# Attention logits from bfloat16 rows that hold three-part splits of the sums, in place of float32 products of diagonals

## The chip, the cores and the metric

The kernel runs on one core of a Trainium2 chip. The metric is the device time of one execution in microseconds (us); a kernel's time is the median of its runs.

In the lines of the profile PE is TensorE (matrix products), DVE VectorE, ACT ScalarE and POOL GpSimd. A line of a timeline gives start and duration in us, engine, source line (L), operation, `output<-inputs`, shapes, and the number of records (x2) that it gathers; `[... <-...]` is the idle time ahead of it, the *idle column*, and what ended it.

## The reference, cut to what matters

Two graph layers over 128 graphs of 64 nodes with 768 features. The change concerns the attention logits of the second layer (6 heads of 128 features):

```python
th = jnp.tanh(h)                                        # h: per head, nodes x 128
attn_src = jnp.einsum('bhno,hoz->bhnz', th, w_src)      # one sum per node and head
attn_dst = jnp.einsum('bhno,hoz->bhnz', th, w_dst)
attn = attn_src + jnp.swapaxes(attn_dst, -1, -2)        # node n, neighbour m
attn = jnp.where(attn >= 0, attn, leaky_alpha * attn)
attn = jnp.where((adj == 0)[:, None, :, :], NEG_MASK, attn)   # NEG_MASK = -999
attn = jax.nn.softmax(attn, axis=-1)
...                                                     # weighted sum, elu, gate
```

So a logit is the sum of a source sum (of the row's node) and a destination sum (of the column's node). The question is how to get 128 x 384 such logits for each tile of two graphs.

## The kernel before

Layer 0 takes the first 1555 us; but for some small constants and transfers it is the same in both kernels. Layer 1 runs over 32 pairs of 128-row tiles. In each of its periods TensorE does the 42 large steps of one pair, each a float32 product with 384 columns, and the small steps of the pair before it are slipped in by step number:

```python
def merged(main, side):            # side steps go in ahead of main step n
    side = sorted(side, key=lambda e: e[0])
    i = 0
    for n, step in enumerate(main):
        while i < len(side) and side[i][0] <= n:
            side[i][1]()
            i += 1
        step()
    ...
```

The steps that the argument touches, with cuts marked by dots:

```python
def heads(t):
    th = work.tile([P, H, DO], F32, name="th")
    nc.scalar.activation(th, HS[t][:, :, :DO], AF.Tanh)
    sd = SD[t] = small.tile([P, 2, H], F32, name="sd")
    for h in range(H):                                   # six destination sums, DVE
        no = work.tile([P, DO], F32, name="no", bufs=1)
        nc.vector.scalar_tensor_tensor(no, th[:, h, :], 1.0, wsd[:, 1, h*DO:(h+1)*DO],
                                       op0=OP.mult, op1=OP.mult,
                                       accum_out=sd[:, 1, h : h + 1])
    dg = PB[t] = work.tile([P, H, N], F32, name="dg")
    for h in range(H):                                   # six diagonals, ACT
        nc.scalar.activation(dg[:, h, :], idc, AF.Copy, scale=sd[:, 1, h : h + 1])
    pr = work.tile([P, H, DO], F32, name="pr", bufs=1)   # source sums: POOL, then DVE
    nc.gpsimd.tensor_mul(pr, th, wsd[:, 0, :].rearrange("p (h o) -> p h o", h=H))
    nc.vector.tensor_reduce(sd[:, 0, :], pr, AX.X, OP.add)

def softmax(t):
    pl = pss.tile([P, H, N], F32, name="ps")
    nc.tensor.matmul(pl, blk, PB[t], start=True, stop=True)      # float32
    a = work.tile([P, H, N], F32, name="a")
    for h in range(H):
        nc.scalar.activation(a[:, h, :], pl[:, h, :], AF.Prelu,
                             bias=SD[t][:, 0, h : h + 1], alpha=LEAKY)
    nc.vector.copy_predicated(a, ...mask..., ...neg...)
    ...                                                  # maximum, subtraction, exp

def final(t, c0=0, c1=D):                                # the "closing operations": four on DVE, 768 columns
    nc.scalar.activation(e, f, AF.Exp, bias=mone)
    nc.vector.scalar_tensor_tensor(f, e, 1.0, f, op0=OP.min, op1=OP.max)
    ...

def behind(p):                                           # (main step, what)
    return [(0, lambda: heads(t0)), (3, lambda: heads(t1)), ...
            (13, lambda: softmax(t0)), (19, lambda: softmax(t1)),
            (24, lambda: turn_p(t0, 0)), ... (39, lambda: final(t1))]
```

Of the kernel before, what the change touches and what calls it, by code (L numbers as in the profile page):

```python
# [8 lines left out]
F32 = mybir.dt.float32  # L9
BF16 = mybir.dt.bfloat16  # L10
I32 = mybir.dt.int32
AF = mybir.ActivationFunctionType
OP = mybir.AluOpType
AX = mybir.AxisListType

P = 128
# [6 lines left out]
def kernel(  # L23
# [106 lines left out]
    ident = const.tile([P, P], F32, name="ident")  # L130
    make_identity(nc, ident)

    blk = const.tile([P, P], F32, name="blk")
    nc.vector.memset(blk, 0.0)

    idc = const.tile([P, N], F32, name="idc")
    for g in range(GT):
        s = slice(g * N, (g + 1) * N)
        nc.vector.memset(blk[s, s], 1.0)
        nc.vector.tensor_copy(idc[s, :], ident[s, s])  # L140
    mhalf = const.tile([P, 1], F32, name="mhalf")
    nc.vector.memset(mhalf, -0.5)

    def stats(src, to, behind=False):

# [62 lines left out]
    with ExitStack() as px:  # L208
# [42 lines left out]
        nc.sync.dma_start(wrt[:, 1, :], wrr_t)  # L251
        identb = wa.tile([P, P], BF16, name="identb")
        nc.vector.tensor_copy(identb, ident)
        blkb = wa.tile([P, P], BF16, name="blkb")
        nc.vector.tensor_copy(blkb, blk)

        vals = wa.tile([P, NG, N], BF16, name="vals")
        nc.gpsimd.iota(vals, pattern=[[1, NG], [0, N]], base=1, channel_multiplier=0,
# [244 lines left out]
        def finish(p):  # L503
            for k in range(2):
                t = 2 * p + k
                to = small.tile([P, 2], F32, name="rn")
                stats(X[t], to)
                h = keep.tile([P, D], F32, name="hf", bufs=2)
                nc.scalar.activation(h, X[t], AF.Relu, scale=to[:, 0:1], bias=to[:, 1:2])
                nc.sync.dma_start(H1D[p][k * P : (k + 1) * P, :], h)  # L510
                nc.gpsimd.tensor_add(X[t], X[t], h)
                nc.sync.dma_start(XH1[p][k * P : (k + 1) * P, :], X[t])
# [40 lines left out]
                (50, lambda: count_t(0, 0)), (50, lambda: count_t(0, 1))]  # L553
        for p in range(NP):
            more = [(3, lambda: finish(p - 1))] if p else late
            if p == NP - 1:
                more += fetch()
            merged(main(p), side(p + 1) + more)


    with ExitStack() as px:
# [16 lines left out]
        def load_x(p):  # L578
            for k in range(2):
                t = 2 * p + k  # L580
                XH[t] = work.tile([P, D], F32, name="x", bufs=4)
                nc.sync.dma_start(XH[t], XH1[p][k * P : (k + 1) * P, :])

        load(0)
# [6 lines left out]
        nc.sync.dma_start(wsd[:, 0, :], row(w_src, P))  # L591
        nc.sync.dma_start(wsd[:, 1, :], row(w_dst, P))
        nc.vector.tensor_scalar(bb, bb, 1.0, None, op0=OP.add)
        neg = wb.tile([P, N], F32, name="neg")
        nc.gpsimd.memset(neg, NEG_MASK)
        mone = wb.tile([P, 1], F32, name="mone")
        nc.gpsimd.memset(mone, -1.0)
        pbds = []
# [2 lines left out]
            nc.gpsimd.memset(pb, 0.0)  # L601
            pbds.append(pb)

        HS, Z, SD, PB = {}, {}, {}, {}
        A11, A12, A22, S1, S2, S3, S4 = {}, {}, {}, {}, {}, {}, {}

        def turn(p, k, h):
# [107 lines left out]
        def heads(t):  # L715

            th = work.tile([P, H, DO], F32, name="th")
            nc.scalar.activation(th, HS[t][:, :, :DO], AF.Tanh)  # L718
            sd = SD[t] = small.tile([P, 2, H], F32, name="sd")
            for h in range(H):  # L720
                no = work.tile([P, DO], F32, name="no", bufs=1)
                nc.vector.scalar_tensor_tensor(no, th[:, h, :], 1.0, wsd[:, 1, h * DO : (h + 1) * DO],  # L722
                                               op0=OP.mult, op1=OP.mult,
                                               accum_out=sd[:, 1, h : h + 1])
            dg = PB[t] = work.tile([P, H, N], F32, name="dg")
            for h in range(H):
                nc.scalar.activation(dg[:, h, :], idc, AF.Copy, scale=sd[:, 1, h : h + 1])  # L727
            pr = work.tile([P, H, DO], F32, name="pr", bufs=1)
            nc.gpsimd.tensor_mul(pr, th, wsd[:, 0, :].rearrange("p (h o) -> p h o", h=H))  # L729
            nc.vector.tensor_reduce(sd[:, 0, :], pr, AX.X, OP.add)  # L730

        def gate(t):

            nc.scalar.activation(Z[t], Z[t], AF.Tanh, scale=0.5)

        def mask(p):

            nc.vector.tensor_scalar(AI[p], AI[p], 0.0, None, op0=OP.is_equal)

        def softmax(t):  # L740

            p, k = divmod(t, 2)
            pl = pss.tile([P, H, N], F32, name="ps")
            nc.tensor.matmul(pl, blk, PB[t], start=True, stop=True)
            a = work.tile([P, H, N], F32, name="a")
            for h in range(H):
                nc.scalar.activation(a[:, h, :], pl[:, h, :], AF.Prelu,
                                     bias=SD[t][:, 0, h : h + 1], alpha=LEAKY)
            nc.vector.copy_predicated(a, AI[p][:, k, None, :].to_broadcast([P, H, N]),
                                      neg[:, None, :].to_broadcast([P, H, N]))  # L750
            mx = small.tile([P, H], F32, name="mx")
            nc.vector.tensor_reduce(mx, a, AX.X, OP.max)
            nc.vector.tensor_sub(a, a, mx[:, :, None].to_broadcast([P, H, N]))
            pb = PB[t] = pbds[t % 2]
            for g in range(GT):
                s = slice(g * N, (g + 1) * N)
                nc.scalar.activation(pb[s, :, s], a[s], AF.Exp)
# [3 lines left out]
        def turn_p(t, q):  # L761
            if q == 0:
                PT[t] = work.tile([P, H, P], F32, name="pT")
            ps = pss.tile([P, KH, P], F32, name="ps")
            for i in range(HH):
                nc.tensor.transpose(ps[:, i, :], PB[t][:, HH * q + i, :], ident)
            nc.scalar.copy(PT[t][:, HH * q : HH * q + HH, :], ps)
# [3 lines left out]
        def attend(t, q):  # L771

            if q == 0:
                FF[t] = work.tile([P, D], F32, name="f")
            po = pss.tile([P, HH, W], F32, name="ps")
            for i in range(HH):
                h = q * HH + i
                nc.tensor.matmul(po[:, i, :], PT[t][:, h, :], HS[t][:, h, :], start=True, stop=True)  # L778
            ri = small.tile([P, HH, 1], F32, name="ri")
            nc.vector.reciprocal(ri, po[:, :, DO : DO + 1])  # L780
            for i in range(HH):
                h = q * HH + i
                nc.vector.scalar_tensor_tensor(FF[t][:, h * DO : (h + 1) * DO], po[:, i, :DO],  # L783
                                               ri[:, i, :], bb, op0=OP.mult, op1=OP.add)
# [24 lines left out]
        def behind(p):  # L809

            if p < 0:
                return []
            t0, t1 = 2 * p, 2 * p + 1
            return [(0, lambda: heads(t0)),
                    (3, lambda: heads(t1)),
                    (5, lambda: load_x(p)),
                    (6, lambda: mask(p)),
                    (6, lambda: gate(t0)),
                    (7, lambda: gate(t1)),
                    (13, lambda: softmax(t0)),  # L820
                    (19, lambda: softmax(t1)),
                    (24, lambda: turn_p(t0, 0)),
                    (26, lambda: turn_p(t0, 1)),
                    (28, lambda: attend(t0, 0)),
                    (30, lambda: attend(t0, 1)),
                    (31, lambda: final(t0)),
                    (32, lambda: turn_p(t1, 0)),
                    (34, lambda: turn_p(t1, 1)),
                    (36, lambda: attend(t1, 0)),
                    (38, lambda: attend(t1, 1)),  # L830
                    (39, lambda: final(t1))]

        def last():


            p = NP - 1
            t0, t1 = 2 * p, 2 * p + 1
            steps = [(21, lambda: heads(t0)),
                     (21, lambda: heads(t1)),
                     (21, lambda: load_x(p)),  # L840
                     (21, lambda: mask(p)),
                     (28, lambda: softmax(t0)),
                     (35, lambda: softmax(t1)),
                     (40, lambda: turn_p(t0, 0)),
                     (40, lambda: turn_p(t0, 1)),
                     (41, lambda: attend(t0, 0)),
                     (41, lambda: attend(t0, 1)),
                     (99, lambda: gate(t0)),
                     (99, lambda: gate(t1))]
            for q in range(2):  # L850
                steps.append((99, lambda q=q: final(t0, q * HALF, (q + 1) * HALF)))
            for q in range(2):
                steps.append((99, lambda q=q: turn_p(t1, q)))
            for q in range(2):
                steps.append((99, lambda q=q: attend(t1, q)))
                steps.append((99, lambda q=q: final(t1, q * HALF, (q + 1) * HALF)))
            return steps
# [55 lines left out]
```

## Time and profile before

| Before | value | how to read it |
|---|---|---|
| time | 2677.28 us (2676.42 to 2678.2) | median of the runs that stand beside the changed kernel |
| TensorE busy | 2620.3 of a 2674.7 us span, 98% | the bound, but its records overlap: only starts can be subtracted |
| period of layer 1 | 34.33 us, 2003.38 to 2037.71 | the same transpose, one pair later |

The lines behind this, and TensorE's waits, are in the prediction.

### The profile page before, as it was taken

What the parts mean: (1) busy time and instruction counts of PE and PEld (TensorE: products, weight loads), DVE (VectorE), ACT (ScalarE), POOL (GpSimd) and SP (SyncE); (2) the same over time, 40 slices, a digit from 0 to 9 for tenths busy, and PEclk for the clock granted to TensorE, in tenths of its full rate; (3) what the DMA queues carried; (4) which work ended last, traced back from release to release, by engine and by line L of the source; (5) the groups of instructions that cost most, each with busy time, mean ns of one, the idle gap of its engine ahead of it and who ended that gap; (6) DMA issues with size and microseconds to landing.
All of it is one profiled execution on the core that took longest, in us unless ns stands there. A gap on an engine that the chain in (4) does not pass through costs nothing.

```text
span 2674.7 us, 29599 instructions
## 1 busy us (share of the span) xinstructions
PE 2620.3 (98%) x10348; PEld 1607.3 (60%) x10348; DVE 1810.1 (68%) x4240; ACT 843.2 (32%) x1892; POOL 612.6 (23%) x657
## 2 busy tenths in 40 slices
PE   6999999999999999999999999999999999999997
PEld 3566566665656656566665566666666666666664
DVE  7865565655646566564655258888888888888878
ACT  1111111111211112121111035555555555555554
POOL 2332222323123232222322221111111111111111
PEclk9999999999999999999999999999999999999998
DMA  5121121211112111121211322222222222222211
GB/s 179 40 75 38 40 73 38 75 38 51 62 38 75 38 65 48 38 75 38 75 36 40 134 86 73 73 73 74 73 73 70 66 68 72 71 65 68 72 61 48
DMA packets 91211, 173.47 MB, mean 65 GB/s; under 512 B 32958, under 2 KB 41521, under 8 KB 91062
## 3 DMA queue, kind: packets, MB, share of 16 engines
q1 hardware_dynamic: 90908, 171.52, 19.4%
q8 instruction: 82, 1.34, 0.2%
q14 instruction: 67, 0.55, 0.1%
q10 hardware_dynamic: 154, 0.06, 0.0%
HBM read 95.67 MB, written 75.50 MB: 64 GB/s over the span
## 4 chain that ended last, share of the span: by engine, by line
PE 71%; DVE 19%; ACT 6%; issue 3%; DMA 1%; SPq 0%; POOL 0%; ACTq 0%; DVEq 0%
PE pwa L451 20%; PE pwb L451 14%; PE pwd L451 7%; PE pwc L451 7%; PE pma L641 5%; PE pb L407 5%; PE pmc L641 5%; DVE no L722 4%; PE pmb L641 3%; DVE f L793 2%; ACT e L792 2%; DVE f L794 2%; DVE f L795 2%; DVE f L783 2%; PE ps L778 2%
## 5 line engine op out<-in xcount | busy, mean ns | idle before, releaser
L451 PE MATMUL pwa<-bwT,s 128*128 128x384 f32 x1152 | 391.1, 489 | 0.4 <-DVE x L468 0.4
L451 PEld LDWEIGHTS pwa<-bwT,s 128*128 128x128 f32 x1152 | 215.1, 190 | 145.4 <-issue 7.4
L641 PE MATMUL pma<-bvT,s 128*128 128x384 f32 x768 | 289.1, 487 | 0.0
L432 POOL TENSOR_TENSOR s<-s,a 128x384 f32<-128x384 f32 x96 | 95.7, 1022 | 644.8 <-PE pwa L451 597.7
L729 POOL TENSOR_TENSOR pr<-th,wsd 128x768 f32<-128x768 f32 x64 | 137.1, 2142 | 418.7 <-ACT th L718 211.2
L468 DVE TENSOR_TENSOR x<-pwa,x 128x384 f32<-128x384 f32 x128 | 69.5, 543 | 206.7 <-PE pwa L451 170.7
L451 PE MATMUL pwb<-bw,s 128*128 128x384 f32 x576 | 201.5, 489 | 0.0
L451 PE MATMUL pwb<-bwT,s 128*128 128x384 f32 x576 | 199.0, 491 | 0.0
L419 ACT COPY a<-pb 128x768 f32<-128x768 f32 x96 | 73.7, 800 | 392.1 <-PE pb L407 392.1
L451 PE MATMUL pwa<-bw,a 128*128 128x384 f32 x576 | 196.8, 490 | 0.0
L451 PE MATMUL pwc<-bw,a 128*128 128x384 f32 x576 | 191.6, 487 | 0.0
L451 PE MATMUL pwd<-bwT,a 128*128 128x384 f32 x576 | 191.3, 486 | 0.0
L396 ACT COPY cntT<-pb 117x128 bf16<-117x128 bf16 (+1 forms) x128 | 27.8, 269 | 484.4 <-PE pb L394 484.4
L727 ACT ACTIVATE dg<-idc,sd 128x64 f32<-128x64 f32 x384 | 128.6, 345 | 124.1 <-DVE no L722 123.8
L407 PE MATMUL pb<-r,h 64*128 64x192 f32 x1536 | 154.4, 341 | 13.2 <-ACT h L316 6.7
L407 PEld LDWEIGHTS pb<-r,h 64*128 64x128 f32 x1536 | 125.2, 190 | 69.2 <-issue 53.0
L641 PEld LDWEIGHTS pma<-bvT,s 128*128 128x128 f32 x768 | 131.5, 191 | 52.6
L722 DVE SCALAR_TENSOR_TENSOR no<-th,wsd 128x128 f32<-128x128 f32 x384 | 152.6, 397 | 5.6 <-ACT th L718 0.9
L451 PEld LDWEIGHTS pwc<-bw,a 128*128 128x128 f32 x576 | 109.8, 191 | 77.1 <-issue 1.5
L451 PEld LDWEIGHTS pwd<-bwT,a 128*128 128x128 f32 x576 | 109.4, 190 | 76.2 <-issue 0.2
L451 PEld LDWEIGHTS pwa<-bw,a 128*128 128x128 f32 x576 | 106.9, 192 | 69.4 <-issue 8.4
L451 PEld LDWEIGHTS pwb<-bwT,s 128*128 128x128 f32 x576 | 106.2, 190 | 69.0 <-issue 6.7
(139 smaller groups left out, 4625.4 us busy)
## 6 DMA issues: line engine op xcount, KB each, us to landing
x<-in_x_dram SPq DMA_DIRECT2D x64, 384.0 KB, 3.7
h<-hf SPq DMA_DIRECT2D x64, 384.0 KB, 3.0
xh<-x SPq DMA_DIRECT2D x64, 384.0 KB
h<-h SPq DMA_DIRECT2D x64, 384.0 KB, 3.0
x<-xh SPq DMA_DIRECT2D x64, 384.0 KB, 3.6
out_dram<-f SPq DMA_DIRECT2D x62, 384.0 KB, 2.6
ai<-in_adj_dram SPq DMA_DIRECT2D x64, 64.0 KB, 2.0
ai<-in_adj_t_dram SPq DMA_DIRECT2D x32, 64.0 KB, 3.4
```

Source lines behind the costliest of these rows:

```text
L407: nc.tensor.matmul(ps[:, g, i * 3 * N : (i + 1) * 3 * N], H0[t][s, kb * P : (kb + 1) * P], rts[p % 2][s, k].rearrange("p s n -> p (s n)"), ...
L419: nc.scalar.copy(A1[p][:, q].rearrange("p h s (g n) -> p g (h s) n", g=GT), pv)
L432: nc.gpsimd.tensor_sub(S2[p][:, q], S1[p][:, q], A1[p][:, q, 0])
L451: nc.tensor.matmul(bank[b][:, :HALF], a()[:, q, s, :], bw[w][s][:, q, :], start=(first and q == s == 0), stop=(q == KH - 1 and s == 2), sk ...
L468: nc.vector.tensor_add(v, bank[b][:, :HALF], v)
L641: nc.tensor.matmul(bank[b, s][:, :HALF], a[p][:, q, :], bv[w][s][:, q, :], start=(first and q == 0), stop=(q == KH - 1), skip_group_check= ...
L722: nc.vector.scalar_tensor_tensor(no, th[:, h, :], 1.0, wsd[:, 1, h * DO : (h + 1) * DO], op0=OP.mult, op1=OP.mult, accum_out=sd[:, 1, h : ...
L727: nc.scalar.activation(dg[:, h, :], idc, AF.Copy, scale=sd[:, 1, h : h + 1])
L729: nc.gpsimd.tensor_mul(pr, th, wsd[:, 0, :].rearrange("p (h o) -> p h o", h=H))
L778: nc.tensor.matmul(po[:, i, :], PT[t][:, h, :], HS[t][:, h, :], start=True, stop=True)
L783: nc.vector.scalar_tensor_tensor(FF[t][:, h * DO : (h + 1) * DO], po[:, i, :DO], ri[:, i, :], bb, op0=OP.mult, op1=OP.add)
L792: nc.scalar.activation(e, f, AF.Exp, bias=mone)
```

## The change

The intent: the float32 logits product costs TensorE four times a bfloat16 one, and ACT spends 12 small instructions per tile on diagonals and biases. Both sums are instead split into three bfloat16 parts (copy, subtract, copy, subtract, copy: three bfloat16 mantissas hold a float32 one), turned into rows by a small bfloat16 product, and one bfloat16 product of 82 rows adds source and destination sums in the float32 accumulator. The mask is done the other way round: a tile is filled with -999 and the edge matrix selects the logits into it. The core of the diff (cuts marked; constants, nine small transfers in layer 0, the order of the last pair and a smaller number of `x` buffers left out):

```diff
 def heads(t):
-            sd = SD[t] = small.tile([P, 2, H], F32, name="sd")
+            pr = work.tile([P, H, DO], F32, name="pr", bufs=1)
+            nc.gpsimd.tensor_mul(pr, th, wsd[:, 0, :]...)          # now first in line
             for h in range(H):
                 ...                                                # six sums on DVE, as before
-            dg = PB[t] = work.tile([P, H, N], F32, name="dg")
-            for h in range(H):
-                nc.scalar.activation(dg[:, h, :], idc, AF.Copy, scale=sd[:, 1, h : h + 1])
-            pr = ...; nc.gpsimd.tensor_mul(pr, ...)
-            nc.vector.tensor_reduce(sd[:, 0, :], pr, AX.X, OP.add)
+            nc.vector.tensor_reduce(sg[:, 2, :], pr, AX.X, OP.add)
+            nc.gpsimd.tensor_mul(sg[:, :GT, :], sd[...], gm[...])
+            sb = sdb[t % 2]
+            for i in range(NPART):                                 # NPART = 3
+                q = sb[:, :, i * H : (i + 1) * H]
+                nc.gpsimd.tensor_copy(q, sg)
+                if i < NPART - 1:
+                    nc.gpsimd.tensor_sub(sg, sg, q)
+        def rows(t):
+            nc.tensor.matmul(ps[:NR, : N + P], sdb[t % 2]..., idr, start=True, stop=True)
+            nc.vector.tensor_mul(rrow[t % 2][: 2 * HB], ps[...], de[: 2 * HB])
+            nc.scalar.copy(lrow[t % 2][2 * HB :], ps[2 * HB : NR, N : N + P])
         def softmax(t):
-            nc.tensor.matmul(pl, blk, PB[t], start=True, stop=True)
-            ...six Prelu with bias, copy_predicated with neg...
+            a = work.tile([P, H, N], F32, name="a")
+            nc.gpsimd.memset(a, NEG_MASK)
+            nc.tensor.matmul(pl, lrow[t % 2], rrow[t % 2], start=True, stop=True)
+            nc.scalar.activation(al, pl, AF.Prelu, alpha=LEAKY)
+            nc.vector.copy_predicated(a, AI[p]..., al)
 def behind(p):
-                    (6, lambda: mask(p)),
-                    (13, lambda: softmax(t0)),
-                    (19, lambda: softmax(t1)),
-                    (24, lambda: turn_p(t0, 0)), ...
+                    (12, lambda: rows(t0)),
+                    (15, lambda: softmax(t0)),
+                    (18, lambda: rows(t1)),
+                    (21, lambda: softmax(t1)),
+                    (25, lambda: turn_p(t0, 0)), ...               # the rest one step later
```

More of the change, by code (lines that the diff above doesn't have):

```diff
@@ L131 @@
     make_identity(nc, ident)
-    blk = const.tile([P, P], F32, name="blk")
-    nc.vector.memset(blk, 0.0)
     idc = const.tile([P, N], F32, name="idc")
@@ L138 @@
         s = slice(g * N, (g + 1) * N)
-        nc.vector.memset(blk[s, s], 1.0)
         nc.vector.tensor_copy(idc[s, :], ident[s, s])
@@ L142, with row_constants @@
     nc.vector.memset(mhalf, -0.5)
+    NPART = 3
+    HB = 32
+    NR = 2 * HB + NPART * H
+    assert NPART * H <= HB
+    dl = const.tile([P, H], F32, name="dl")
+    nc.gpsimd.memset(dl, 0.0)
+    def row_constants():
+        for c in range(3):
+            for i in range(NPART):
+                a = c * HB + i * H
+                nc.sync.dma_start(dl[a : a + H, :], ident[0:H, 0:H])
     def stats(src, to, behind=False):
@@ L254 @@
         blkb = wa.tile([P, P], BF16, name="blkb")
-        nc.vector.tensor_copy(blkb, blk)
+        nc.vector.memset(blkb, 0.0)
+        for g in range(GT):
+            s = slice(g * N, (g + 1) * N)
+            nc.vector.memset(blkb[s, s], 1.0)
         vals = wa.tile([P, NG, N], BF16, name="vals")
@@ L555 @@
             more = [(3, lambda: finish(p - 1))] if p else late
+            if p == 1:
+                more.append((10, row_constants))
             if p == NP - 1:
@@ L580, in load_x @@
                 t = 2 * p + k
-                XH[t] = work.tile([P, D], F32, name="x", bufs=4)
+                XH[t] = work.tile([P, D], F32, name="x", bufs=3)
                 nc.sync.dma_start(XH[t], XH1[p][k * P : (k + 1) * P, :])
@@ L593 @@
         nc.vector.tensor_scalar(bb, bb, 1.0, None, op0=OP.add)
-        neg = wb.tile([P, N], F32, name="neg")
-        nc.gpsimd.memset(neg, NEG_MASK)
         mone = wb.tile([P, 1], F32, name="mone")
@@ L602 @@
             pbds.append(pb)
-        HS, Z, SD, PB = {}, {}, {}, {}
+        de = wb.tile([P, H, N], BF16, name="de")
+        nc.gpsimd.tensor_copy(de, dl[:, :, None].to_broadcast([P, H, N]))
+        idr = wb.tile([P, N + P], BF16, name="idr")
+        nc.gpsimd.tensor_copy(idr[:, :N], idc)
+        nc.gpsimd.tensor_copy(idr[:, N:], ident)
+        gm = wb.tile([P, GT], F32, name="gm")
+        nc.gpsimd.memset(gm, 0.0)
+        for g in range(GT):
+            nc.gpsimd.memset(gm[g * N : (g + 1) * N, g : g + 1], 1.0)
+        lrow, rrow, sdb = [], [], []
+        for i in range(2):
+            sb = wb.tile([P, 3, HB], BF16, name=f"sdb{i}")
+            nc.gpsimd.memset(sb, 0.0)
+            sdb.append(sb)
+            rr = wb.tile([NR, H, N], BF16, name=f"rrow{i}")
+            nc.gpsimd.tensor_copy(rr[2 * HB :], de[2 * HB : NR])
+            rrow.append(rr)
+            lr = wb.tile([NR, P], BF16, name=f"lrow{i}")
+            nc.gpsimd.memset(lr, 0.0)
+            for g in range(GT):
+                nc.gpsimd.memset(lr[g * HB : (g + 1) * HB, g * N : (g + 1) * N], 1.0)
+            lrow.append(lr)
+        HS, Z, PB = {}, {}, {}
         A11, A12, A22, S1, S2, S3, S4 = {}, {}, {}, {}, {}, {}, {}
@@ L718, in heads @@
             nc.scalar.activation(th, HS[t][:, :, :DO], AF.Tanh)
-            sd = SD[t] = small.tile([P, 2, H], F32, name="sd")
+            pr = work.tile([P, H, DO], F32, name="pr", bufs=1)
+            nc.gpsimd.tensor_mul(pr, th, wsd[:, 0, :].rearrange("p (h o) -> p h o", h=H))
+            sd = small.tile([P, H], F32, name="sd")
+            sg = small.tile([P, 3, H], F32, name="sg")
             for h in range(H):
@@ L722, in heads @@
                 nc.vector.scalar_tensor_tensor(no, th[:, h, :], 1.0, wsd[:, 1, h * DO : (h + 1) * DO],
-                                               op0=OP.mult, op1=OP.mult,
-                                               accum_out=sd[:, 1, h : h + 1])
-            dg = PB[t] = work.tile([P, H, N], F32, name="dg")
-            for h in range(H):
-                nc.scalar.activation(dg[:, h, :], idc, AF.Copy, scale=sd[:, 1, h : h + 1])
-            pr = work.tile([P, H, DO], F32, name="pr", bufs=1)
@@ L729, in heads @@
-            nc.gpsimd.tensor_mul(pr, th, wsd[:, 0, :].rearrange("p (h o) -> p h o", h=H))
-            nc.vector.tensor_reduce(sd[:, 0, :], pr, AX.X, OP.add)
+                                               op0=OP.mult, op1=OP.mult, accum_out=sd[:, h : h + 1])
+            nc.vector.tensor_reduce(sg[:, 2, :], pr, AX.X, OP.add)
+            nc.gpsimd.tensor_mul(sg[:, :GT, :], sd[:, None, :].to_broadcast([P, GT, H]),
+                                 gm[:, :, None].to_broadcast([P, GT, H]))
+            sb = sdb[t % 2]
@@ new lines, in heads @@
+            for i in range(NPART):
+                q = sb[:, :, i * H : (i + 1) * H]
[3 more added lines that the diff above has]
+        def rows(t):
+            ps = pss.tile([P, KH, P], F32, name="ps").rearrange("p a b -> p (a b)")
+            nc.tensor.matmul(ps[:NR, : N + P], sdb[t % 2].rearrange("p c v -> p (c v)")[:, :NR], idr,
+                             start=True, stop=True)
+            nc.vector.tensor_mul(rrow[t % 2][: 2 * HB],
+                                 ps[: 2 * HB, None, :N].to_broadcast([2 * HB, H, N]), de[: 2 * HB])
+            nc.scalar.copy(lrow[t % 2][2 * HB :], ps[2 * HB : NR, N : N + P])
@@ L732, in gate @@
         def gate(t):
             nc.scalar.activation(Z[t], Z[t], AF.Tanh, scale=0.5)
-        def mask(p):
-            nc.vector.tensor_scalar(AI[p], AI[p], 0.0, None, op0=OP.is_equal)
         def softmax(t):
             p, k = divmod(t, 2)
+            a = work.tile([P, H, N], F32, name="a")
+            nc.gpsimd.memset(a, NEG_MASK)
             pl = pss.tile([P, H, N], F32, name="ps")
-            nc.tensor.matmul(pl, blk, PB[t], start=True, stop=True)
-            a = work.tile([P, H, N], F32, name="a")
-            for h in range(H):
-                nc.scalar.activation(a[:, h, :], pl[:, h, :], AF.Prelu,
-                                     bias=SD[t][:, 0, h : h + 1], alpha=LEAKY)
-            nc.vector.copy_predicated(a, AI[p][:, k, None, :].to_broadcast([P, H, N]),
-                                      neg[:, None, :].to_broadcast([P, H, N]))
+            nc.tensor.matmul(pl, lrow[t % 2], rrow[t % 2], start=True, stop=True)
@@ L751, in softmax @@
+            al = work.tile([P, H, N], F32, name="al", bufs=1)
+            nc.scalar.activation(al, pl, AF.Prelu, alpha=LEAKY)
+            nc.vector.copy_predicated(a, AI[p][:, k, None, :].to_broadcast([P, H, N]), al)
             mx = small.tile([P, H], F32, name="mx")
@@ L816, in behind @@
                     (5, lambda: load_x(p)),
-                    (6, lambda: mask(p)),
                     (6, lambda: gate(t0)),
                     (7, lambda: gate(t1)),
-                    (13, lambda: softmax(t0)),
-                    (19, lambda: softmax(t1)),
-                    (24, lambda: turn_p(t0, 0)),
-                    (26, lambda: turn_p(t0, 1)),
-                    (28, lambda: attend(t0, 0)),
-                    (30, lambda: attend(t0, 1)),
-                    (31, lambda: final(t0)),
-                    (32, lambda: turn_p(t1, 0)),
-                    (34, lambda: turn_p(t1, 1)),
-                    (36, lambda: attend(t1, 0)),
-                    (38, lambda: attend(t1, 1)),
-                    (39, lambda: final(t1))]
+                    (12, lambda: rows(t0)),
+                    (15, lambda: softmax(t0)),
+                    (18, lambda: rows(t1)),
+                    (21, lambda: softmax(t1)),
+                    (25, lambda: turn_p(t0, 0)),
+                    (27, lambda: turn_p(t0, 1)),
+                    (29, lambda: attend(t0, 0)),
+                    (31, lambda: attend(t0, 1)),
+                    (32, lambda: final(t0)),
+                    (33, lambda: turn_p(t1, 0)),
+                    (35, lambda: turn_p(t1, 1)),
+                    (37, lambda: attend(t1, 0)),
+                    (39, lambda: attend(t1, 1)),
+                    (40, lambda: final(t1))]
         def last():
@@ L840, in last @@
                      (21, lambda: load_x(p)),
-                     (21, lambda: mask(p)),
-                     (28, lambda: softmax(t0)),
-                     (35, lambda: softmax(t1)),
+                     (30, lambda: rows(t0)),
+                     (33, lambda: softmax(t0)),
+                     (36, lambda: rows(t1)),
+                     (38, lambda: softmax(t1)),
                      (40, lambda: turn_p(t0, 0)),
```

## The prediction

> **What bounds the kernel now.** I read the page first: engine totals and the 40 slices.
>
> ```profile
> PE 2620.3 (98%) x10348; PEld 1607.3 (60%) x10348; DVE 1810.1 (68%) x4240; ACT 843.2 (32%) x1892; POOL 612.6 (23%) x657
> ...
> PE   6999999999999999999999999999999999999997
> ...
> DVE  7865565655646566564655258888888888888878
> ACT  1111111111211112121111035555555555555554
> ```
>
> TensorE is full except at both ends. The change touches only layer 1, the slices from about 1560 us on, where DVE is at 80% and ACT at 50%. Next, who TensorE waited for from 1500 us to the end (longest entries):
>
> ```profile
> PE ps L612 <- ACT a L747: 8.3, 29, 0.3
> PE ps L766 <- DVE ri L780: 3.3, 1, 3.3
> PE ps L744 <- ACT dg L727: 2.8, 3, 2.4
> ```
>
> So the 31 periods of layer 1, one per pair of tiles, are set by TensorE's own work plus one 0.29 us wait. One period, from TensorE's timeline:
>
> ```profile
> 2003.38 0.49 PE L612 MATMUL ps<-ident,h 128*128 128x128 f32 x3
> ...
> 2005.02 0.91 PE L744 MATMUL ps<-dg,blk 128*128 128x384 f32 x2
> 2005.77 0.81 PE L641 MATMUL pma<-bvT,s 128*128 128x384 f32 x2
> ...
> 2009.13 0.55 PE L612 MATMUL ps<-ident,h 128*128 128x128 f32 x3 [0.29 <-ACT a L747]
> ...
> 2010.81 0.81 PE L744 MATMUL ps<-dg,blk 128*128 128x384 f32 x2
> ...
> 2037.71 0.49 PE L612 MATMUL ps<-ident,h 128*128 128x128 f32 x3
> ```
>
> The same transpose comes at 2003.38 and at 2037.71: a period is 34.33 us. Take starts, not durations, which hold pipeline latency: a pair of 384-column float32 records advances by 0.645 us (0.65 at 2010.81), the first logits product by 0.75, because its operand came just in time. That is the important point: the wait is small, but the slack behind it is nil.
>
> DVE and POOL show what fills the time before that product:
>
> ```profile
> 2001.52 0.95 DVE L730 TENSOR_REDUCE sd<-pr 128x6 f32<-128x768 f32 x1
> ...
> 2003.06 1.51 DVE L722 SCALAR_TENSOR_TENSOR no<-th,wsd 128x128 f32<-128x128 f32 x1
> 2004.51 0.07 DVE L722 DVE_READ_ACCUMULATOR no<-th,wsd 128x1 f32 x1
> ```
>
> ```profile
> 2002.62 1.81 POOL L729 TENSOR_TENSOR pr<-th,wsd 128x768 f32<-128x768 f32 x1 [6.80 <-DVE sd L730]
> ```
>
> The last of the six row sums of the first tile takes 1.51 instead of 0.28 us and ends just after POOL's product ends (2004.43). The next ACT copy makes the last diagonal (`dg`, ended 4.97), and the product starts at 5.02.
>
> **What the Trainium skill says.** (1) "TensorE: Matmul & The Clock Gate", section Back-to-back issue gap: N/2.4 + 2.5 ns per warm product, 162.5 ns for 384 columns. The trace agrees: two bf16 products of 384 columns (the counts, L460) advance by 0.33 us together (1509.03 to 1509.36), and a float32 one costs four times 0.16. (2) "SBUF — State Buffer", section Who interferes with whom: a DVE instruction with two SBUF inputs and a GpSimd instruction that reads SBUF exclude each other for the whole instruction. The 1.51 us above agrees, 29 us of the `ai` compare (0.91 each) likewise. (3) "ScalarE: Activation LUTs", section What ACT_TABLE_LOAD costs: an ACTIVATE with immediate operands is 186 + 0.833 N ns, so an estimated 0.51 us for the one 384-wide Prelu; the trace has 0.48 to 0.50 for copies of that width.
>
> **The change part by part.**
>
> *TensorE, per pair.* Removed: two float32 logits products, 0.75 + 0.645 = 1.40. Added: two bf16 products of 384 columns, 2 x 0.163, and two of 192 columns that turn the sums into rows: 0.08 each by the formula, I take 0.10 because the next weight load is only partly hidden. Together 0.53. Saved 0.87. The 0.29 wait at the transpose should go too: it was for the six Prelus of 0.316 (their bank), now one of 0.5. A period without new waits: 34.33 - 0.87 - 0.29 = 33.17. Over 31 periods that is 36 us.
>
> *ACT, per tile.* Six `dg` (0.345) and six Prelus (0.316) go, one Prelu (0.5) and one 18x128 copy (0.27, as L396) come: 4.0 becomes 0.8, some 200 us in all. ACT is at 50%, so nothing directly.
>
> *DVE.* The compare of `ai` goes (29 us), 64 products into the bf16 rows come (0.55 x 64 = 35). Even.
>
> *POOL, per tile.* A 128x384 memset (about 0.42 by the 0.744 of 768 columns) and a chain of six dependent small ones, multiply, copy, subtract, copy, subtract, copy, which makes the three parts. From TENSOR_TENSOR at 384 (1.00) and 768 columns (1.81) the fixed part is 0.19, so about 0.22 for 18 columns; copies about 0.15 (L386: 0.40 for 243); gaps between dependent POOL instructions 0.08 (1557.55 + 0.99 to 1558.62). Estimate: 3 x 0.22 + 3 x 0.15 + 5 x 0.08 = 1.5; with hand-overs from DVE (0.15) and to the weight load (0.1), 1.75.
>
> *Where it lies.* I took the instruction orders of the changed kernel and laid one period out by hand with these durations. Let E be the end of a pair's last product. TensorE wants the first rows product at E + 8.07 (twelve steps of 0.645 plus a transpose group of 0.33). DVE after E: z add at 0.20, a row sum 0.66, `sg` reduce 0.87, the first of the closing operations at 1.74 to 2.69. POOL's second `pr` is ready at 2.75 but blocked by it, runs to 4.37 and holds back the next row sum. Then sum, closing, sum and so on, 3.03 (1998.28 to 2001.31), so the sixth sum starts at 7.48 and its accumulator is out at 7.77. Plus 1.75: the parts are there at E + 9.5, wanted at about 8.0. TensorE waits 1.5 us in each period. `pr` of the second tile stands ahead of the chain in POOL's order, so there is no way round.
>
> From rows to logits: the DVE product (about 10.3 to 10.9) and the ACT copy (10.9 to 11.2) are in time for 12.1. Second tile: `a` is filled on POOL only behind the second chain (about 13.9), so copy, maximum, subtraction, z add and then the second row product reach 16.7, exponentials and copy 17.2; wanted 16.9. Another 0.3 us.
>
> Sum per period: 33.17 + 1.5 + 0.3 = 35.0, or +0.65 x 31 = +20 us. The tail (from 2606 us, a DVE chain) loses some `dg` and Prelu time and gains two POOL chains: 0 to +4. Set-up of the constants on POOL at about 1550 to 1557: some 20 small instructions, 4 us, before S2 that was needed only at 1564.18: hidden. Nine small DMAs in layer 0: hidden. Together 2678 + 20 + 2 = 2700.
>
> **The rivals.**
> 1. *The chain fits, only the saving remains:* 2678 - 36 = 2642. For it: TensorE is the bound and the steps were moved by one, which looks tuned. Against: the slack was nil before, the rows product is wanted one step (0.645) earlier, and a 1.75 us chain is added while the sixth sum comes only 0.5 us earlier. Partial versions, with faster small POOL instructions, lie between.
> 2. *A lost race adds more.* POOL's first `pr` starts 1.57 after the hs add that its tanh waits for (2026.04 to 2027.61), the last closing operation 1.44 after (2027.48); DVE wins by 0.13. If it now waits for an attention product that is a step later and POOL goes first, DVE loses 1.75 us more per period: 2700 + 54 = 2754.
> 3. *DVE as the bound:* 80% before and about the same after, with 35 us periods; no.
> 4. *x with three buffers:* the reused tile's last reader is a period earlier; no wait expected.
>
> **Range and chances.** I give rival 1 and its partial forms 40%, my layout 40%, rival 2 20%. That pulls the prediction slightly below the layout: 2695 us, 2645 to 2755. Even the full saving is 1.3%, so over 2% faster is nearly excluded (0.02). Slower than 2731 needs the lost race or a much longer chain: 0.22. Within 2%: 0.76.
>
> **What would show it.** Right: TensorE waits of 1 to 2 us at the first rows product, put down to POOL, about 31 times; a period near 35 us; no wait at the transpose for Prelu; six small POOL instructions near 1.5 us from first start to last end; a long row sum beside the second `pr`. Wrong: a period near 33.2 with no wait at the rows product (rival 1), or a closing operation of some 2.7 us beside the first `pr` and a period near 37 (rival 2). If the period is near 33.2 and the total is not, the loss is in the tail or at the change of layers.

## The result, and the profile after

The changed kernel takes 2686.48 us (2685.72 to 2687.96, four runs) against 2677.28: the ratio is 1.0035, with a 95% interval of 1.0018 to 1.0052. It is some 9 us slower, well inside 2%. Each 95% interval excludes 1, so the small differences are real. The ratios lie nearer to the ratio of the mean times than to that of the medians.

The engine totals of the changed kernel:

```profile
PE 2592.6 (97%) x10348; PEld 1591.5 (59%) x10348; DVE 1832.4 (68%) x4271; ACT 704.0 (26%) x1252; POOL 744.0 (28%) x1121
```

ACT lost 139 us and POOL gained 131, and TensorE is 28 us *less* busy in a span that is 9 us longer. (That its number of records is unchanged is a coincidence: two float32 records per tile became two bfloat16 ones.) So TensorE waits somewhere. Whom it waited for from 1500 us to the end, as totals, number of waits and longest:

```profile
PE ps L782 <- POOL sdb L774: 45.1, 31, 3.3
PE ps L818 <- DVE f L835: 2.8, 1, 2.8
PE ps L830 <- ACT pT L819: 1.3, 2, 0.7
PE ps L798 <- ACT lrow L786: 1.2, 1, 1.2
```

L782 is the rows product and L774 the last copy of POOL's split. It has 31 waits (29 of 1.38, and 1.71 and 3.32 in the last period); the 8.3 us of waits at the transpose are gone. One period on TensorE's timeline (start, duration, what, and the idle time ahead of it):

```profile
2003.17 1.45 PE L682 MATMUL pma<-bv,a 128*128 128x384 f32 x4
...
2006.98 0.28 PE L782 MATMUL ps<-idr,sdb 128*82 128x192 bf16 x1 [1.38 <-POOL sdb L774]
...
2009.39 0.33 PE L798 MATMUL ps<-rrow,lrow 82*128 82x384 bf16 x1
2009.56 1.45 PE L682 MATMUL pmc<-bv,a 128*128 128x384 f32 x4
...
2031.91 2.10 PE L682 MATMUL pma<-bv,a 128*128 128x384 f32 x6
...
2037.71 0.49 PE L682 MATMUL pma<-bv,a 128*128 128x384 f32 x1
```

The product at 2003.17 comes again at 2037.71: the period is 34.54 us, 0.21 longer than before. The logits product now costs 0.17 us (2009.39 to 2009.56) and doesn't wait, and one wait of 1.38 stands ahead of the rows product. The main products of this pair start at 2031.91 − 34.54 = 1997.37, which is the prediction's E.

What held the rows product back, on DVE and then on POOL:

```profile
1999.11 0.95 DVE L845 SCALAR_TENSOR_TENSOR f<-e,f 128x768 f32<-128x768 f32 x1
1999.97 1.90 DVE L766 SCALAR_TENSOR_TENSOR no<-th,wsd 128x128 f32<-128x128 f32 x1
...
2004.84 0.28 DVE L766 SCALAR_TENSOR_TENSOR no<-th,wsd 128x128 f32<-128x128 f32 x1
2005.05 0.08 DVE L766 DVE_READ_ACCUMULATOR no<-th,wsd 128x1 f32 x1
```

```profile
1999.34 2.39 POOL L761 TENSOR_TENSOR pr<-th,wsd 128x768 f32<-128x768 f32 x1 [2.75 <-ACT z L790]
2005.20 0.21 POOL L769 TENSOR_TENSOR sg<-sd,gm 128x12 f32<-128x12 f32 x1 [3.48 <-DVE no L766]
2005.48 0.20 POOL L774 CAST sdb<-sg 128x18 bf16<-128x18 f32 x1
...
2006.62 0.31 POOL L774 CAST sdb<-sg 128x18 bf16<-128x18 f32 x1
```

Read them together. POOL issues its second `pr` at 1999.34, while DVE is in the first closing operation; its record lasts 2.39 us, where the second `pr` of the kernel before took 1.81. So I read that it can't run until the closing operation ends, and then goes ahead of DVE's third row sum, which stands for 1.90 us instead of 0.28. That sum ends 0.14 after `pr` (1999.34 + 2.39 = 2001.73). The sixth sum is at 2004.84, its accumulator is out at 2005.13, and the six small POOL instructions then follow one another, 2005.20 to 2006.93. The rows product starts 0.05 us after the last of them.

The spans differ by 9.2 us (2683.9 against 2674.7). To see where, I cut both traces at the same two transposes, one in the second period of layer 1 and one 29 periods later. The first comes at 1599.70 before and at 1598.68 after, the second at 2595.92 and at 2600.47. So the stretch up to the first changed by −1.0 us, the 29 periods by +5.6 (996.22 became 1001.79), and the last stretch, the tail, by +4.6 (78.8 became 83.4).

### The profile page after: what moved, and what is told of

It reads as the page before. It is cut to its first block, busy times and chain, and to the rows that moved or that the text cites. A ratio compares the mean times of both kernels' runs of the same rounds, so it can differ in the third digit from the quotient of the medians. Undisturbed runs are those within 1.5% of the kernel's fastest.

```text
span 2683.9 us, 29514 instructions
## 1 busy us (share of the span) xinstructions
PE 2592.6 (97%) x10348; PEld 1591.5 (59%) x10348; DVE 1832.4 (68%) x4271; ACT 704.0 (26%) x1252; POOL 744.0 (28%) x1121
## 4 chain that ended last, share of the span: by engine, by line
PE 72%; DVE 21%; issue 3%; POOL 2%; ACT 1%; DMA 1%; SPq 0%; ACTq 0%; DVEq 0%
PE pwa L467 20%; PE pwb L467 14%; PE pwd L467 7%; PE pma L682 7%; PE pwc L467 6%; PE pb L423 5%; PE pmc L682 5%; DVE f L835 4%; DVE no L766 3%; PE pmb L682 3%; DVE f L845 2%; DVE f L846 2%; DVE z L716 2%; DVE hs L716 2%; PE ps L653 1%
## 5 line engine op out<-in xcount | busy, mean ns | idle before, releaser
L761 POOL TENSOR_TENSOR pr<-th,wsd 128x768 f32<-128x768 f32 x64 | 154.3, 2410 | 257.9 <-ACT th L759 172.1
L766 DVE SCALAR_TENSOR_TENSOR no<-th,wsd 128x128 f32<-128x128 f32 x384 | 161.5, 421 | 4.4 <-ACT th L759 1.9
L467 PEld LDWEIGHTS pwb<-bw,s 128*128 128x128 f32 x576 | 106.1, 190 | 61.8
```

The source lines that it names most:

```text
L467: nc.tensor.matmul(bank[b][:, :HALF], a()[:, q, s, :], bw[w][s][:, q, :], start=(first and q == s == 0), stop=(q == KH - 1 and s == 2), sk ...
```

## The experiments

Eight kernels in two calls, each timed beside the kernel before on the same chip (2677.81 us in the first call, 2678.11 in the second). The theory from the prediction: TensorE's rows product waits for a chain on DVE and POOL, the chain is long because six small POOL instructions follow the last row sum and because `pr` holds up one row sum, and TensorE's own saving is real but hidden behind that wait. The rivals: (A) bfloat16 products between float32 ones cost TensorE time that no wait shows; (B) DVE, at about 80%, is the real bound and any removed wait comes back as another; (C) the collision of `pr` with DVE's row sum plays no part, and the added POOL instructions alone are the cause.

All eight were reported as agreeing with the reference, even the two that are wrong. The comparison therefore says nothing on the exactness of the logits.

**1. Take the wait away.** POOL does all its work, but the parts go to a tile that nobody reads; the rows product reads parts that were set to zero once. Its output is wrong, which doesn't matter for the time.

```diff
+        sdx = wb.tile([P, 3, HB], BF16, name="sdx")
-            sb = sdb[t % 2]
+            sb = sdx
```

> Wrong result on purpose: the six small POOL instructions write their parts into a tile that nobody reads, and the rows product takes zero parts filled once. All instructions stay; only the dependency of the rows product on the chain goes. Theory (the loss is the wait of the first rows product for the sixth row sum plus the POOL chain): the 1.38 us wait there goes in all periods. What is left is the next thing in line, the bf16 row product on DVE behind the row sums and the ACT copy after it, which end at most 0.4 us too late for the logits product, so the period falls from 34.54 to 33.2 to 33.6 us and the time to 2642 to 2658. Rival A (mixing bf16 with float32 products costs TensorE time of its own): 2686 within 4. Rival B (DVE at over 80% is now the bound): 2686 within 4.

Measured: 2655.76 us, ratio 0.9918 (0.9903 to 0.9933), as expected. The wait at the rows product is gone, and a smaller one appears at the logits product, for a row that comes from ACT. Its entry in TensorE's waits (the lines are one further down in this kernel):

```profile
PE ps L799 <- ACT lrow L787: 12.8, 31, 1.2
```

The sum closes: 45.1 us of waits went, 12.8 − 1.2 = 11.6 came there, and the tail has a new 2.9 us one for DVE, which leaves 30.6; the times differ by 30.7. Rivals A and B would have kept the time near 2686: both fall for the size of the loss.

**2 and 3. Shorten POOL's chain.** One part or two instead of three, which rounds the sums.

```diff
-    NPART = 3
+    NPART = 1        # and 2 in the other kernel
```

> Inexact result on purpose: one bfloat16 part of the sums in place of three, so the POOL chain is two instructions in place of six (the rows product has 70 columns of weights in place of 82, the logits product 70 rows). Theory: the parts come four instructions of about 0.28 us earlier, 1.1 us, so of the 1.38 us wait 0.25 to 0.3 stays, the DVE row product may hold the logits product for 0.1 to 0.3 more: 2686 - 31 x 0.8 to 1.1 = 2652 to 2661. Rivals A and B: 2686 within 4.

> Two parts in place of three: two POOL instructions fewer, 0.57 us. Theory: the wait at the first rows product falls from 1.38 to 0.8 us and the time by 31 x 0.57 = 18 us, to 2669 within 3; a dose between the change and one part. Rivals A and B: 2686 within 4. The result should still pass a bfloat16 comparison, as two parts hold 16 bits.

Measured: one part 2653.37 us (ratio 0.9909, 0.9893 to 0.9926), inside what was expected. The idle column names no wait in its loop, but a rest of it is there by starts:

```profile
2019.95 2.10 PE L682 MATMUL pma<-bv,a 128*128 128x384 f32 x6
...
2028.32 0.27 PE L782 MATMUL ps<-idr,sdb 128*70 128x192 bf16 x1
...
2030.08 0.81 PE L682 MATMUL pma<-bvT,s 128*128 128x384 f32 x2
2030.95 0.34 PE L798 MATMUL ps<-rrow,lrow 70*128 70x384 bf16 x1
```

The rows product comes 8.37 after the pair's main products, 0.30 later than the 8.07 of an unhindered one, and the logits product is held up by another 0.22 (0.87 after a pair of records that takes 0.645). Both were expected. Two parts 2664.28 (0.995, 0.9935 to 0.9965), some 2 us below the range that was expected, mainly in the tail: the wait in each period fell by 0.68 (1.38 to 0.70), which is 20 of the 22 us over 29 periods. POOL's two small instructions that go cost 0.28 each from start to start, so 0.57; TensorE's wait shrank by slightly more. By starts the rows product is late by 1.54, 0.86 and 0.30 us with three, two and one parts: it follows the length of POOL's chain almost us for us, to the end. The total gains 22.2 us by the first step and only 10.9 by the second, mainly because the logits product is then the one that is late.

**4. Ask for the result later.** The same work and the same chain, but the side steps that need it are two to four main steps later.

```diff
-                    (12, lambda: rows(t0)),
-                    (15, lambda: softmax(t0)),
-                    (18, lambda: rows(t1)),
-                    (21, lambda: softmax(t1)),
+                    (14, lambda: rows(t0)),
+                    (18, lambda: softmax(t0)),
+                    (20, lambda: rows(t1)),
+                    (25, lambda: softmax(t1)),
```

> Same work, exact result: the rows product of the first tile two steps later (14), its logits at step 18, the second tile at 20 and 25. Theory: the rows product is wanted at about E + 9.7 us and its parts are there at 9.5, so the wait goes without taking any work away; the exponentials had 3.6 us to spare before the transposes. Period 33.2 us, time 2642 to 2650, which would beat both kernels. If instead the exponentials then come late for the transposes, a wait of up to 1 us shows there and the time is 2650 to 2680. Rivals A and B: 2686 within 4.

Measured: 2640.75 us (2639.38 to 2641.78), ratio 0.9862 (0.9847 to 0.9877), slightly below the range. The two waits for POOL that are left stand in the last period, one for the pair before the last (0.42) and one for the last pair:

```profile
PE ps L782 <- POOL sdb L774: 4.0, 2, 3.6
```

On the timeline the rows product now starts without idle time ahead of it, and the blocked row sum is still there, first line TensorE, second DVE:

```profile
2022.79 0.25 PE L782 MATMUL ps<-idr,sdb 128*82 128x192 bf16 x1
```

```profile
2015.72 1.90 DVE L766 SCALAR_TENSOR_TENSOR no<-th,wsd 128x128 f32<-128x128 f32 x1
```

The pair's main products start at 2013.10, so the rows product comes 9.69 us after them, and POOL's last copy ended at 2022.67, 9.57 after them. The chain is as long as it was; it is only asked for when it is ready. The period is 32.96 us (1999.76 to 2032.72, two transposes of the same kind).

**5. The same for the old form.** A control: was it the change that gained, or the spacing?

```diff
-                    (13, lambda: softmax(t0)),
-                    (19, lambda: softmax(t1)),
+                    (15, lambda: softmax(t0)),
+                    (21, lambda: softmax(t1)),
```

> Control: the kernel before (float32 logits) with only the steps moved, its two logits products at steps 15 and 21 in place of 13 and 19. It tells how much of the gain of the fourth run is spacing that the old form could have had too. Theory: the old form waits only 0.1 us at its first logits product and 0.29 us at a transpose per period, so 0.1 to 0.4 us x 31 is all there is: 2665 to 2675. TensorE's own work for the float32 logits (0.87 us per period more) stays. Rival (the gain was all spacing): 2641 within 5.

Measured: 2659.52 us (2659.2 to 2660.86), ratio 0.9934 (0.992 to 0.9947), better than expected. Later steps alone take 18.6 us off the old kernel. Its period is 33.71, from these two lines of TensorE's timeline:

```profile
2004.38 0.81 PE L744 MATMUL ps<-dg,blk 128*128 128x384 f32 x2
...
2038.09 0.81 PE L744 MATMUL ps<-dg,blk 128*128 128x384 f32 x2
```

That is 0.62 less than 34.33, although the profile of the kernel before shows an idle time of only 0.29 at the transpose. I expected 3 to 13 us and 18.6 came, because I took the idle column at its word. By starts, the transpose was held up by 0.45 and the first logits product by 0.12. With both forms spaced well, the change is worth 33.71 − 32.96 = 0.75 us per period, and that is TensorE's own work.

**6. Take the collision away by a second buffer.** The second `pr` waits for the first to be read; with two buffers it could run earlier. Memory for it comes from `x`.

```diff
-                XH[t] = work.tile([P, D], F32, name="x", bufs=3)
+                XH[t] = work.tile([P, D], F32, name="x", bufs=2)
-            pr = work.tile([P, H, DO], F32, name="pr", bufs=1)
+            pr = work.tile([P, H, DO], F32, name="pr", bufs=2)
```

> Exact result: two buffers for POOL's product pr in place of one (x goes to two buffers to make room, its readers are a period apart), steps as in the change. The second pr then need not wait for the reduce of the first and runs beside PSUM-fed operations of DVE, before the third row sum. Theory (that sum's 1.9 us beside the second pr is what makes the chain late): the sixth sum comes about 1.1 us earlier, the wait at the first rows product falls from 1.38 to about 0.3 us, 2686 - 31 x 1.1 = 2652, range 2645 to 2662. Rival C (the POOL chain alone, not the lock, makes the wait): 2686 within 5.

Measured: 2682.95 us, ratio 1.0022 (1.0008 to 1.0036). A clear miss, and the number lies where rival C put it (2686 within 5); the lines and run 7 decide. POOL's timeline, then DVE's, of this kernel:

```profile
2027.50 4.28 POOL L761 TENSOR_TENSOR pr<-th,wsd 128x768 f32<-128x768 f32 x2 [5.40 <-ACT th L759]
```

```profile
2030.05 1.88 DVE L766 SCALAR_TENSOR_TENSOR no<-th,wsd 128x128 f32<-128x128 f32 x1
```

The second `pr` follows the first without a gap, up to 2031.78, and now it is the *first* row sum that meets it and stands for 1.88 us. The third is back at 0.28. The sixth sum starts 7.41 us after the pair's main products (2030.86 to 2038.27), against 7.47 with one buffer. The collision moved along the same chain and was not removed, so the wait at the rows product stays at 1.32. This run alone doesn't separate the theory from rival C.

**7. Take the collision away by taking the product away.** The odd tile reuses the even tile's `pr`. Wrong; all twelve small POOL instructions per pair stay.

```diff
-            pr = work.tile([P, H, DO], F32, name="pr", bufs=1)
-            nc.gpsimd.tensor_mul(pr, th, ...)
+            if t % 2 == 0:
+                PR[0] = work.tile([P, H, DO], F32, name="pr", bufs=1)
+                nc.gpsimd.tensor_mul(PR[0], th, ...)
+            pr = PR[0]
```

> Wrong result on purpose: the odd tile reduces the even tile's pr, so the second POOL product of 1.8 us is gone and nothing else. Steps as in the change. Theory: the long row sum beside it falls from 1.9 to 0.28 us, the parts come 1.65 us earlier, more than the 1.38 us wait, and the row products on DVE come earlier with them: no wait, period 33.2 us, 2642 to 2647. Rival C: 2686 within 5, as all six small POOL instructions are there.

Measured: 2635.81 us (2634.51 to 2636.69), ratio 0.9844 (0.983 to 0.9857), below what was expected: the period is 32.97 us (the transpose at 1624.63 comes again at 2020.23, twelve periods later) and not 33.2, and in the tail TensorE waits 1.6 us for POOL in place of 5.0. The third row sum of a period in this kernel, on DVE, and the rows product, on TensorE:

```profile
2015.74 0.28 DVE L768 SCALAR_TENSOR_TENSOR no<-th,wsd 128x128 f32<-128x128 f32 x1
```

```profile
2021.20 0.25 PE L784 MATMUL ps<-idr,sdb 128*82 128x192 bf16 x1
```

The main products start at 2013.13, so the rows product is at 8.07 us after them, exactly where the prediction said that TensorE wants it. Without the 1.6 us that `pr` takes from DVE, the full chain of six POOL instructions fits, which refutes rival C. The cause is the two together: without the collision all of the delay goes (this run); with it, a shorter POOL chain takes it down to 0.86 or 0.30 us by starts (runs 3 and 2).

**8. The best version.** Run 4, with the last pair's steps later as well. It computes what the changed kernel does, in another order.

```diff
 behind(p): as in run 4
 last():
-                     (30, lambda: rows(t0)),
-                     (33, lambda: softmax(t0)),
-                     (36, lambda: rows(t1)),
-                     (38, lambda: softmax(t1)),
-                     (40, lambda: turn_p(t0, 0)), (40, lambda: turn_p(t0, 1)),
-                     (41, lambda: attend(t0, 0)), (41, lambda: attend(t0, 1)),
+                     (36, lambda: rows(t0)),
+                     (38, lambda: softmax(t0)),
+                     (39, lambda: rows(t1)),
+                     (41, lambda: softmax(t1)),
+                     (41, lambda: turn_p(t0, 0)), (41, lambda: turn_p(t0, 1)),
+                     (42, lambda: attend(t0, 0)), (42, lambda: attend(t0, 1)),
```

> The fourth run plus the last pair's steps: its rows at 36 and 39 in place of 30 and 36, its logits at 38 and 41. In the fourth run TensorE waited 3.6 us at that rows product with six products still behind it. Theory: it does those products first; 0 to 4 us less than the fourth run, 2636 to 2641. Rival D (the tail is set by the DVE and POOL chain alone): 2641 within 1.5.

Measured: 2635.09 us (2634.64 to 2635.71, five runs), 0.9 below the range, ratio 0.9842 (0.9828 to 0.9855): 1.6% faster than the kernel before, 1.9% than the changed one. The largest of TensorE's waits from 1500 us on, all in the last period or behind it:

```profile
PE ps L818 <- DVE f L835: 4.1, 2, 2.1
PE ps L798 <- ACT lrow L786: 3.6, 1, 3.6
...
PE ps L782 <- POOL sdb L774: 0.4, 1, 0.4
```

The wait for POOL is nearly gone and those for DVE and ACT at the end are longer than in run 4 (2.8 and 1.2); on balance the span is 4.4 us shorter.

In the idle column a delay reads some 0.16 us too short (see the last section). All runs in order of time:

| kernel | us | ratio to before | idle column at the rows product, per period |
|---|---|---|---|
| 8, later steps, tail too | 2635.09 | 0.9842 | none |
| 7, one `pr` per pair (wrong) | 2635.81 | 0.9844 | none |
| 4, later steps | 2640.75 | 0.9862 | none |
| 2, one part | 2653.37 | 0.9909 | none, but 0.30 late by starts |
| 1, zero parts (wrong) | 2655.76 | 0.9918 | none |
| 5, before, later steps | 2659.52 | 0.9934 | has no rows product |
| 3, two parts | 2664.28 | 0.995 | 0.70 |
| before | 2677.28 | 1 | has no rows product |
| 6, two `pr` buffers | 2682.95 | 1.0022 | 1.32 |
| changed | 2686.48 | 1.0035 | 1.38 |

## Why the prediction was right or wrong

The time on record was 2695, the result 2686.48: inside the range and in the likeliest class. The mechanism was the one laid out; one term of the sum was not there, and one small one was mis-sized.

- **The layout of DVE up to the sixth sum held** to 0.01 us: first closing operation at E + 1.74 (predicted 1.74), end of the second `pr` at E + 4.36 (4.37), sixth sum at E + 7.47 (7.48), accumulator out at E + 7.76 (7.77).
- **POOL's chain** took 1.73 from its first start to its last end against 1.5 plus margins of 0.25 for hand-overs. The small instructions are slower than guessed (a copy 0.20, not 0.15) and the hand-overs faster (0.07 and 0.05). The errors cancel in part: 1.85 in all against 1.75.
- **The wait at the rows product**: predicted 1.5, started at E + 9.61 instead of E + 8.07, so 1.54. The profile's idle column says 1.38, because it is counted from the modelled end of the product before it.
- **The failed step: "Another 0.3 us" at the second tile's logits product.** The prediction put the memset of `a` behind the second POOL chain of the same period and made DVE wait for it. There is no such wait. Two lines, DVE and POOL of the changed kernel:

```profile
2010.49 0.59 DVE L802 COPY_PREDICATED a<-ai,al 128x384 f32<-128x384 int32 x1 [1.60 <-ACT al L800]
```

```profile
2013.41 0.42 POOL L796 MEMSET a<- 128x384 f32 x1 [2.83 <-ACT pbd L809]
```

  The selection waits for ACT's Prelu, not for POOL, and the fill comes *after* it: as soon as the exponentials have read a buffer of `a`, POOL fills it for its next use. `a` has two buffers, so the fill serves the same tile of the next pair. I had placed the memset by its rank in POOL's order and forgotten which use of the buffer it serves. That is 0.3 x 31 = 9 us too much.
- **The mis-sized term: the period without new waits**, 33.17 predicted. Starts give 34.54 − 1.54 = 33.0, and run 4, which has no wait in the loop, 32.96. The missing 0.17 is in the 0.29 of the transpose: by starts it was 0.45 (run 5). The prediction warned that durations hold latency and then took an idle time that was derived from such a duration. Another 5 us too much.
- **TensorE's own saving**, 0.87 with 0.11 of it a late start, so 0.76 of work: run 5 against run 4 gives 0.75.
- **The tail**: predicted 0 to +4, came out at +4.6. Two POOL chains stand in TensorE's way in the last period, one of the pair before the last and one of the last pair, with waits of 1.71 and 3.32 us; these are inside the 45.1 us above.
- **The rivals.** Rival 1 (the chain fits) got 40% and did not happen in the changed kernel, but its 2642 is what run 4 shows once the steps are spaced for the chain: 2640.75. Rival 2 (the lost race) did not happen: the last closing operation still starts 0.12 us ahead of POOL's first `pr`, 2028.42 against 2028.54; the prediction had 0.13. Rival 3 (DVE as the bound) is refuted by runs 4, 7 and 8, where DVE does its work in a shorter time. Rival 4 (a wait for `x`): none appears, not even with two buffers in run 6.

From the layout's 2700 to the result: −9 for the wait that isn't there, −5 for the period, +1 for the longer rows wait, +3 for the tail, and −1 for the first period, which has no wait; that is 2689. Of the remaining 2 to 3 us 0.7 is the base (2678 taken, 2677.28 measured); the rest was not traced.

What the shading to 2695 did was to move the number towards the result, by chance: it was put there for partial forms of rival 1, and none of them occurred.

What stays open: whether the three parts are needed for the accuracy that this kernel wants. The comparison with the reference passes with one part and even with zeros, so it cannot tell.

## What to carry to other kernels

A product that starts 0.1 us late for want of its operand has no slack behind it: a change that makes the product cheaper but its operands later turns into a wait of the full length, here 1.54 us lost against 1.33 saved in each period. So when a change lengthens a chain on engines that look idle (POOL at 23%), lay out that chain from its source to the moment when the bound engine asks for it, with the instructions that exclude each other; and after such a change, move the asking before changing the chain, because that cost one edit of four numbers and gave back 46 us. Give the old form the same tuning before crediting the change: of the 37 us between the kernel before and run 4 (2677.81 to 2640.75), later steps alone give the old form 18.6.

## What the Trainium skill lacked or had wrong

- "SBUF — State Buffer", section Who interferes with whom: it says that the one that issues first holds the shared pair for the whole instruction, which the traces agree with. It doesn't say expressly who gets it next when one engine waits for it and the other, which holds it, has more of the same in its queue. Here DVE held it for a closing operation, POOL's `pr` began to wait at 1999.34, and POOL went ahead of DVE's next two-input sum, which began at 1999.97 and stood for 1.90 us instead of 0.28. The records fit "first asked, first served"; no run here tests it by itself.
- "GPSIMD Engine Reference", section 3.1, the table of measured numbers: it has one size, 2048 columns, and no time of a small GPSIMD instruction as a whole. Here 12 to 18 columns took 0.20 to 0.22 us (0.31 for the last copy), and 0.28 from start to start in a dependent chain. That is the figure that decides such a chain.
- "Perfetto Trace Analysis", section Tensor Engine Instruction (MATMUL, LD_WEIGHTS): it says that the end of a TensorE record is an estimate, but not what that does to idle times. Here a float32 record of 384 columns lasts 0.49 us where starts are 0.323 apart, so an idle time ahead of a product reads 0.16 us too short: 1.38 for a delay of 1.54, and 0.29 for one of 0.45.
